# Fewer, larger transfers for the experts of a mixture-of-experts layer: two weight loads a part, one load of all biases, one output store, and a reordered hand-over

## The chip, the cores and the metric

The kernel runs on one core of one Trainium2 chip. Its time is device time in microseconds (us) of one execution, the median of several runs. A core has a matrix engine (TensorE, PE; its weight loads are listed as PEld), a vector engine (VectorE, DVE), a scalar engine (ScalarE, ACT), GpSimd (POOL) and a queue engine (SyncE, SP), each with its own instruction stream, and 16 DMA engines, which are fed from queues of SP, ACT and POOL. "Tile" below is a buffer in on-chip memory; "PSUM" is the memory that PE writes to.

## The reference

The input x has 32 images of 56 x 56 tokens of 128 channels, in float32. It goes through a binarised 3 x 3 convolution with group and batch normalisation, a windowed causal attention with 4 heads, and a mixture-of-experts layer in which every expert chooses its tokens. The change touches only this last layer:

```
logits = einsum('bsd,ed->bse', x, gate_w) + gate_b
probs = softmax(logits, axis=1)                       # over the 3136 tokens of an image
vals, idx = top_k(probs.transpose(0, 2, 1), K)        # 64 experts, K = 8 tokens each
gathered = take_along_axis(x, flat_idx[:, :, None], axis=1)
pooled = einsum('bked,bke->bed', gathered, topv)      # one vector per image and expert
h = gelu(einsum('ebd,edh->ebh', [pooled, 1], weight1))  # 512 hidden values
out = einsum('ebh,eho->ebo', [h, 1], weight2)
weighted = einsum('beo,bke->bkeo', out, topv)
outputs = zeros.at[batch, flat_idx].add(weighted)     # added onto the layer's input
```

x is the layer-normalised input here. A token that several experts of one image chose gets the sum of their outputs. weight1 is 64 x 129 x 512 and weight2 is 64 x 513 x 128; the last row of each is the bias. Together they are 33.6 MB.

## The kernel before

**Main loop.** The images are taken in 16 pairs (NPAIR), and the tokens of a pair in 7 blocks, so that there are N = 112 blocks. One loop over n runs the whole chain (load, convolution, normalisation, attention, projection) as a pipeline written out by hand: in one turn different blocks are at different stages. Each engine's order is the order of the code, apart from waits on semaphores. The normalised tokens of a pair are stored to `toks` in DRAM, the layer's residual to the output.

**Choosing tokens.** As soon as a pair's blocks are through, `Pair.step(j)` runs one step a block: `spread` sends the inverse deviations through DRAM into `drow` (a row per expert), `scale` multiplies the logits by them, `largest` and `tokens` take the 8 largest and their indices (`idx`, `idxf`) and store them (`slots`, `putrow`), `gather` fetches the 8 token rows with eight indirect DMAs of POOL into `rows`. `row_stats` stores these rows to `grows` in DRAM with 16 DMAs on SP (L804), computes their statistics, and loads `srow`, the indices of all experts of the image in each partition (L817). `weigh` makes the weighted sum `g_acc` of the rows, which `turn_pooled` and `pool` turn into `pooled`. `shares` compares `srow` with a slot's index, eight times (L854, L859): how much each expert adds to the token of each slot. `store_shares` stores this to `share` in DRAM by a DMA of POOL. `put_rows` loads `rowidx`, the output rows of all slots.

**Hand-over.** For the last pair these steps come after the loop, one behind the other, with the first loads for the experts among them.

**Experts.** The 64 experts are taken in 16 groups of 4 (NG, EG), two groups to a part, 8 parts (NQ). `Group(g, pool)` loads the group's weights on SP: four DMAs of 256 KB for u1 (L353), four for u2 (L355), four of 16 KB for the biases u3 (L360). The pools `early` and `late` hold two groups each, so four groups, two parts, are in flight; group g + 4 is loaded at the end of `outputs(g)`. For a part q the code runs:

- `hidden(g)`: hp = pooled x u1, 16 products (L1019); ACT copies it to `hs` (L1024);
- `gelus(g)`: transposes (L1030) and 32 activations with the first bias (L1035);
- `outputs(g)`: op = hT x u2 (L1047), DVE adds the second bias into `os` (L1054), ACT stores it to `eout` in DRAM (L1055), and after the second group loads the part's outputs back into `eo` in an order by image (L1061). `eo` lies in a tile named logits, and the profile calls it so;
- `finals(q)`: for each pair fo = share x eo (L1072), DVE adds it to the token rows `f_rows` (L1077), and 16 indirect DMAs of POOL scatter them into the output (L1081).

`finals(q - 1)` stands between `gelus` and `outputs` of part q. `load_rows` (L1005) and `load_shares` (L1013) bring a part's `f_rows` and `f_sh` from `grows` and `share`, two parts ahead.

Scatters of one pair stay in the order of the parts. POOL, PE, DVE, ACT and SP otherwise wait only for data and for buffers.

Of the kernel before, what the change touches and what calls it, by code (L numbers as in the profile page):

```python
# [17 lines left out]
P = 128  # L18
# [3 lines left out]
K = 8  # L22
# [8 lines left out]
def kernel(  # L31
# [303 lines left out]
    grows = dram.tile([NQ, P, NPAIR, P], F32, name="grows")  # L335
# [8 lines left out]
    class Group:  # L344


        def __init__(self, g, pool):
            self.e0 = g * EG
            self.u1 = pool.tile([P, EG, HF], F32, name="u1")
            self.u2 = pool.tile([P, EG, NHC, P], F32, name="u2")  # L350
            self.bias = pool.tile([P, P], F32, name="u3")
            for e in range(EG):
                nc.sync.dma_start(out=self.u1[:, e, :], in_=weight1[self.e0 + e, 0:C, :])  # L353
            for e in range(EG):
                nc.sync.dma_start(  # L355
                    out=self.u2[:, e].rearrange("p c o -> p (c o)"),
                    in_=weight2[self.e0 + e, 0:HF, :].rearrange("(p c) o -> p (c o)", c=NHC),
                )
            for e in range(EG):
                nc.sync.dma_start(  # L360
                    out=self.bias[e * B : (e + 1) * B],
                    in_=weight2[g * EG + e, HF : HF + 1, :].to_broadcast([B, P]),
                )
# [3 lines left out]
    def main_loop(fast):  # L367
        with ExitStack() as main:
# [7 lines left out]
            early = main.enter_context(tc.tile_pool(name="early", bufs=2))  # L376
# [324 lines left out]
            class Pair:  # L701
# [48 lines left out]
                def tokens(self):  # L750
# [18 lines left out]
                    nc.sync.dma_start(out=slots[pr], in_=self.idxf)  # L769
                    nc.sync.dma_start(out=putrow[pr], in_=pidx)  # L770
# [28 lines left out]
                def row_stats(self):  # L799

                    pr, rows = self.pr, self.rows
                    for i in range(2):
                        for q in range(NQ):
                            nc.sync.dma_start(  # L804
                                out=grows[q, i * ES : (i + 1) * ES, pr, :].rearrange(
                                    "(e k) c -> e k c", k=K
                                ),
                                in_=rows[i * E + q * EP : i * E + (q + 1) * EP],
                            )
# [4 lines left out]
                    self.srow = wp.tile([P, E, K], F32, name="srow")  # L814
                    for i in range(2):
                        half = slice(i * E, (i + 1) * E)
                        nc.sync.dma_start(  # L817
                            out=self.srow[half].rearrange("p e k -> p (e k)"),
                            in_=slots[pr][half].rearrange("(o e) k -> o (e k)", o=1).to_broadcast([E, E * K]),
                        )  # L820

                def weigh(self):

                    rows, st = self.rows, self.st
                    rtot = wp.tile([P, 1], F32, name="rtot")
                    nc.vector.reciprocal(rtot, self.tot)
                    nc.vector.tensor_scalar(self.topv, self.topv, rtot, None, ALU.mult)
# [49 lines left out]
                def step(self, j):  # L877
# [11 lines left out]
                    elif j == 6:  # L889
                        self.row_stats()  # L890
                    elif j == 7:
                        self.weigh()
# [20 lines left out]
            for n in range(-6, N + 1):  # L913
# [12 lines left out]
                if n == N - 4:  # L926
                    groups = [Group(g, early) for g in range(2)]
# [31 lines left out]
                for j, pair in steps:  # L959
                    pair.step(j)  # L960
# [19 lines left out]
            def pool(name, bufs, space=None):  # L980
# [4 lines left out]
                pool(name, bufs) for name, bufs in (("late", 2), ("eh", 2), ("frow", 4), ("fsh", 1))  # L985
# [11 lines left out]
            sync_dep = mybir.DependencyInfo(mybir.DependencyClass.Sync, mybir.DependencyReason.DATA)  # L997

            def load_rows(q, n0, n1):
# [3 lines left out]
                for a in range(n0, n1, FP):  # L1003
                    b = min(a + FP, n1)
                    nc.sync.dma_start(out=rows[q][:, a:b], in_=grows[q][:, a:b])  # L1005

            def load_shares(q, n0, n1):
                shs[q] = shbuf[q % 3]
                for i in range(2):
                    part = slice(i * E, (i + 1) * E)  # L1010
                    for a in range(n0, n1, 2 * FP):
                        b = min(a + 2 * FP, n1)
                        nc.sync.dma_start(out=shs[q][part, a:b, i, :], in_=share[q][part, a:b])  # L1013

            def hidden(g):
                group = groups[g]
                hp = eps.tile([P, HF], F32, name="hp")
                for e in range(EG):
                    nc.tensor.matmul(  # L1019
                        hp[e * B : (e + 1) * B, :], lhsT=pooled[:, group.e0 + e, :],  # L1020
                        rhs=group.u1[:, e, :], start=True, stop=True,
                    )
                hs[g] = eh.tile([P, HF], F32, name="hs")
                nc.scalar.copy(hs[g], hp)  # L1024

            def gelus(g):
                hT_ps = eps.tile([P, NHC, P], F32, name="hT_ps")
                hc = hs[g].rearrange("p (m c) -> p c m", c=NHC)
                for c in range(NHC):
                    nc.tensor.transpose(hT_ps[:, c, :], hc[:, c, :], ident)  # L1030
                hT[g] = eh.tile([P, NHC, P], F32, name="hT")
                for c in range(NHC):
                    for e in range(EG):
# [159 lines left out]
```

## Time and profile before

| | us |
|---|---|
| median of 3 runs (lowest and highest) | 2401.21 (2399.71 to 2408.39) |
| profiled execution | 2529.53 |
| its span in the profile | 2527.7 |
| main loop, about | 280 to 2150 |
| hand-over | 2170 to 2244 |
| experts, from the first fo to the end | 2244 to 2528 |
| start of `finals` of parts 0 to 7 | 2243.7, 2277.9, 2311.5, 2344.9, 2384.3, 2427.3, 2471.0, 2497.7 |
| busy in the span: PE, DVE, ACT, POOL | 2198.1, 1770.1, 1166.8, 812.6 |

All times within the kernel are from one profiled execution, counted from the start of its span. It is 128 us longer than the median of the runs. In the views, a row of waits reads: engine and line that waited, "<-", the engine and the line (or the DMA) that ended the wait, the sum in us, how often, the longest. Rows of SPq, ACTq and POOLq are the DMA issues of a queue: start, how long the issuing took, line, target and source, number.

### The profile page before, as it was taken

What the parts mean: (1) busy time and instruction counts of PE and PEld (TensorE: products, weight loads), DVE (VectorE), ACT (ScalarE), POOL (GpSimd) and SP (SyncE); (2) the same over time, 40 slices, a digit from 0 to 9 for tenths busy, and PEclk for the clock granted to TensorE, in tenths of its full rate; (3) what the DMA queues carried; (4) which work ended last, traced back from release to release, by engine and by line L of the source; (5) the groups of instructions that cost most, each with busy time, mean ns of one, the idle gap of its engine ahead of it and who ended that gap; (6) DMA issues with size and microseconds to landing.
All of it is one profiled execution on the core that took longest, in us unless ns stands there. A gap on an engine that the chain in (4) does not pass through costs nothing.

```text
span 2527.7 us, 83568 instructions
## 1 busy us (share of the span) xinstructions
PE 2198.1 (87%) x35852; PEld 1527.2 (60%) x35852; DVE 1770.1 (70%) x4955; ACT 1166.8 (46%) x1699; POOL 812.6 (32%) x761
## 2 busy tenths in 40 slices
PE   6769999999999999999999999999999999234433
PEld 5647676666666666666666666666666666123212
DVE  8965577878787878787878787878788787621101
ACT  0015555555555555555555555565555554122211
POOL 1011223232424242423333333333232424324434
PEclk9989999999999999999999999999999999667766
DMA  9932344443435353434343435353534445755552
GB/s 374 391 108 55 94 108 104 105 113 95 122 87 137 79 130 83 126 86 126 92 117 93 125 88 133 77 132 82 126 91 117 100 108 141 193 163 181 168 152 83
DMA packets 272749, 321.22 MB, mean 127 GB/s; under 512 B 74801, under 2 KB 214257, under 8 KB 270321
## 3 DMA queue, kind: packets, MB, share of 16 engines
q1 hardware_dynamic: 240496, 241.29, 34.1%
q0 software_dynamic: 27392, 72.38, 11.4%
q8 instruction: 285, 4.67, 0.8%
q10 hardware_dynamic: 4480, 2.10, 0.3%
q14 instruction: 96, 0.78, 0.1%
HBM read 190.35 MB, written 125.31 MB: 125 GB/s over the span
## 4 chain that ended last, share of the span: by engine, by line
PE 71%; issue 10%; ACT 7%; POOL 6%; DVE 6%; DMA 0%; POOLq 0%; SPq 0%; another core or an unknown queue 0%; DVEq 0%
PE cv L503 8%; PE av L633 8%; PE kT_ps L544 8%; PE pj L667 7%; PE v_ps L560 7%; PE sc L584 6%; POOL out_dram L1081 4%; PE xT_ps L434 4%; PE lg L695 4%; PE yt L434 4%; ACT bn L482 4%; PE rr L531 4%; PE tt L434 3%; ACT xT L474 3%; DVE st L301 3%
## 5 line engine op out<-in xcount | busy, mean ns | idle before, releaser
L420 POOL TENSOR_TENSOR ln_rstd<-ln_var,nhalf 128x7 f32<-128x7 f32 x112 | 167.6, 1497 | 946.1 <-DVE ln_var L417 607.7
L474 ACT ACTIVATE xT<-xT_ps,conv_nb 128x896 f32<-128x896 f32 x112 | 112.8, 1007 | 401.6 <-PE xT_ps L434 401.6
L420 POOL TENSOR_TENSOR devs<-ln_var,nhalf 128x7 f32<-128x7 f32 x112 | 165.8, 1480 | 267.5 <-DVE ln_var L417 267.5
L503 PE MATMUL cv<-hbits,wconv 128*128 128x448 f16 x1008 | 236.3, 361 | 12.4 <-DVE s L518 6.3
L599 ACT ACTIVATE pT<-sc 128x896 f32<-128x896 f32 x224 | 193.3, 915 | 115.8 <-PE sc L584 115.8
L633 PEld LDWEIGHTS av<-vblk,pT 64*64 64x64 f32 x12544 | 194.4, 135 | 80.1 <-ACT pT L599 72.9
L560 PEld LDWEIGHTS v_ps<-wqkvT,n1T 128*128 128x128 f32 x1568 | 192.7, 192 | 41.6 <-issue 41.6
L633 PE MATMUL av<-vblk,pT 64*64 64x33 f32 x12544 | 207.6, 221 | 0.8 <-ACT pT L599 0.5
L673 DVE SCALAR_TENSOR_TENSOR tT<-pj,bproj_c,yT 128x448 f32<-128x448 f32 x224 | 142.7, 679 | 92.7 <-PE pj L667 70.9
L516 ACT ACTIVATE s<-cv,conv_mid 128x448 int32<-128x448 f32 x112 | 70.8, 632 | 295.9 <-PE cv L503 219.6
L544 PE MATMUL kT_ps<-n1T,wqkvT 128*128 128x448 f32 x448 | 197.8, 564 | 4.4
L667 PE MATMUL pj<-aoT,wprojT 64*128 64x448 f32 x896 | 200.3, 566 | 1.1 <-ACT aoT L659 1.1
L560 PE MATMUL v_ps<-wqkvT,n1T 128*128 128x128 f32 x1568 | 193.1, 275 | 0.0
L544 PE MATMUL qT_ps<-n1T,wqkvT 128*128 128x448 f32 x448 | 187.7, 542 | 0.0
L427 DVE BATCH_NORM_STATS2 ln_st<-yt 128x6 f32<-128x128 f32 x784 | 165.6, 285 | 22.0 <-PE tt L434 9.6
L1081 POOL DMA_INDIRECT out_dram<-f_rows,rowidx x128 | 123.8, 967 | 165.7 <-DVE f_rows L1077 129.1
L584 PE MATMUL sc<-qT,kT 32*64 32x64 f32 x12544 | 172.0, 237 | 2.1 <-issue 2.1
L584 PEld LDWEIGHTS sc<-qT,kT 32*64 32x64 f32 x12544 | 156.0, 133 | 25.8 <-issue 25.7
L686 POOL DMA_DIRECT2D out_dram<-tok x224 | 169.3, 757 | 0.0
L427 DVE BATCH_NORM_STATS2 ln_st<-tok 128x6 f32<-128x128 f32 x784 | 161.9, 281 | 5.2 <-ACT tok L681 5.2
L482 ACT ACTIVATE bn<-xT_ps,thr_b,thr_a 128x448 f32<-128x448 f32 x224 | 149.2, 720 | 3.1 <-DVE thr_b L330 2.6
L520 DVE SCALAR_TENSOR_TENSOR yT<-s,conv_s,xT 128x448 f32<-128x448 f32 x224 | 143.5, 682 | 4.0
(183 smaller groups left out, 4105.3 us busy)
## 6 DMA issues: line engine op xcount, KB each, us to landing
xb<-in_x_dram SPq DMA_DIRECT2D x16, 3136.0 KB
xb<-in_x_dram SPq DMA_DIRECT2D x224, 224.0 KB
toks<-tok SPq DMA_DIRECT2D x224, 224.0 KB
out_dram<-tok POOLq DMA_DIRECT2D x224, 224.0 KB
u<-in_L_ffn_weight_dram SPq DMA_DIRECT2D x128, 256.0 KB
drow<-devs SPq DMA_DIRECT2D x224, 112.0 KB
grows<-rows SPq DMA_DIRECT2D x256, 32.0 KB
f_rows<-grows SPq DMA_DIRECT2D x30, 256.0 KB
```

What stands on the lines that cost most here:

```text
L420: nc.gpsimd.tensor_tensor(rstd, var, nhalf[:, :n], ALU.pow)
L427: nc.vector.bn_stats(st[:, u, :], src[:, u, :])
L434: nc.tensor.transpose(units(t)[:, u, :], src[:, u, :], ident)
L482: nc.scalar.activation(bn[:, i].rearrange("c h (g j) -> c h g j", j=NU), units(xT_ps)[:, :, i * WIN : (i + 1) * WIN].rearrange("c j (h g) ...
L503: nc.tensor.matmul(self.cv[:, :BT], lhsT=wconv[:, t, :], rhs=hb[:, r * RB + kh : r * RB + kh + RB, kw : kw + W], start=(t == 0), stop=(t = ...
L544: nc.tensor.matmul(pp[:, a, :BT], lhsT=wqkvT[:, s, :], rhs=flat[:, a * BT : (a + 1) * BT], start=True, stop=True,)
L560: nc.tensor.matmul(units(vp)[:, u, :], lhsT=self.n1T[:, u, :], rhs=wqkvT[:, 2, :], start=True, stop=True,)
L584: nc.tensor.matmul(tiles[h // 2][part, h % 2, u * WIN : (u + 1) * WIN], lhsT=left[hp, u, part], rhs=right[hp, u, part], start=False, stop= ...
L599: nc.scalar.activation(pT, rows2(sc), AF.Exp, scale=HD ** -0.5)
L633: nc.tensor.matmul(av[h % 2 * WIN : (h % 2 + 1) * WIN, i, m * VW : (m + 1) * VW], lhsT=self.pT[h // 2][rows, h % 2, u, :], rhs=self.vb[row ...
L667: nc.tensor.matmul(pj[:, i, :BT], lhsT=wprojT[rows, g, :], rhs=self.aoT[rows, :, g, :], start=(g == 0), stop=(g == 1),)
L1081: put = nc.gpsimd.indirect_dma_start(out=of, out_offset=bass.IndirectOffsetOnAxis(ap=rowidx[:, n, q : q + 1], axis=0), in_=rows[q][:, n, : ...
```

## The change

- **Weights.** `Part(q, pool)` takes the place of `Group`. It loads a part's u1 in one DMA of 2 MB and its u2 in another. Each of the pools `early` and `late` holds one part. u1 of part q + 2 is issued after `hidden(q)`, u2 after `outputs(q)`.
- **Biases.** All second biases are loaded once, with four DMAs in the hand-over, into `obias`, which lies in the buffer of `drow`.
- **Outputs.** `hidden`, `gelus` and `outputs` take a part. `os` holds both groups and is stored to `eout` by one DMA of 128 KB.
- **Rows and shares.** `grows` is laid out by slot, and a pair's rows are stored in one DMA, for every pair. A part's `f_rows` come in two DMAs, with runs of up to 8 KB, its `f_sh` in two.
- **Last pair.** In the last turn of the loop the steps of the pairs run in reverse order. In the hand-over `slot_rows` (the load of `srow`) follows the store of `slots` at once; five of the eight shares come before the weighted sum; three after `hidden(0)`; most memsets of POOL come ahead of the gathers; `put_rows` comes last. `probabilities` holds two instructions that were in `weigh`.

```
-    grows = dram.tile([NQ, P, NPAIR, P], F32, name="grows")
+    grows = dram.tile([P, K, NPAIR, P], F32, name="grows")
...
+    class Part:
+        def __init__(self, q, pool):
+            self.q, self.pool = q, pool
+        def load1(self):
+            self.u1 = self.pool.tile([P, EP, HF], F32, name="u1")
+            es = slice(self.q * EP, (self.q + 1) * EP)
+            nc.sync.dma_start(out=self.u1, in_=weight1[es, 0:C, :].rearrange("e c h -> c e h"))
+        def load2(self):
+            self.u2 = self.pool.tile([P, EP, NHC, P], F32, name="u2")
+            es = slice(self.q * EP, (self.q + 1) * EP)
+            nc.sync.dma_start(
+                out=self.u2.rearrange("p e c o -> p e (c o)"),
+                in_=weight2[es, 0:HF, :].rearrange("e (p c) o -> p e (c o)", c=NHC),
+            )
...
                     nc.sync.dma_start(out=slots[pr], in_=self.idxf)
+                    if pr == NPAIR - 1:
+                        self.slot_rows()
                     nc.sync.dma_start(out=putrow[pr], in_=pidx)
...
-                    for i in range(2):
-                        for q in range(NQ):
-                            nc.sync.dma_start(
-                                out=grows[q, i * ES : (i + 1) * ES, pr, :].rearrange(
-                                    "(e k) c -> e k c", k=K
-                                ),
-                                in_=rows[i * E + q * EP : i * E + (q + 1) * EP],
-                            )
+                    nc.sync.dma_start(out=grows[:, :, pr, :], in_=rows)
...
                 if n == N - 4:
-                    groups = [Group(g, early) for g in range(2)]
+                    parts = [Part(0, early)]
+                    parts[0].load1()
+                    parts[0].load2()
...
-                for j, pair in steps:
+                for j, pair in steps if n < N else steps[::-1]:
                     pair.step(j)
...
+                for i in range(2):
+                    es = slice(i * E + q * EP, i * E + (q + 1) * EP)
+                    nc.sync.dma_start(
+                        out=rows[q][i * ES : (i + 1) * ES, n0:n1],
+                        in_=grows[es].rearrange("e k n c -> (e k) n c")[:, n0:n1],
+                    )
...
+            def outputs(q):
+                part = parts[q]
+                os = eh.tile([P, GQ, P], F32, name="os")
+                for g in range(q * GQ, (q + 1) * GQ):
...
+                    for e in range(EG):
+                        one = slice(e * B, (e + 1) * B)
+                        nc.vector.tensor_add(os[one, g % GQ], op[one, e % 2, :], obias[one, g])
+                es = slice(q * EP, (q + 1) * EP)
                 nc.scalar.dma_start(
-                    out=eout[group.e0 : group.e0 + EG].rearrange("e b o -> (e b) o"), in_=os
+                    out=eout[es].rearrange("(g e) b o -> (e b) g o", e=EG), in_=os
                 )
...
-                if g + 4 < NG:
-                    groups.append(Group(g + 4, early if g % 4 < 2 else late))
...
+            parts[1].load1()
+            parts[1].load2()
             pair.scale(NB - 1, NB)
             pair.largest(NB - 1, NB)
+            nc.gpsimd.memset(eo, 0.0)
+            zeros(0)
+            zeros(1)
             pair.tokens()
             pair.gather()
-            pair.put_rows()
-            pairs[NPAIR - 2].shares(range(2, 8))
-            pairs[NPAIR - 2].store_shares()
-            for q in range(2):
+            other.shares(range(2, 8))
+            other.store_shares()
+            for q in range(3):
                 load_rows(q, 0, N1)
-                load_shares(q, 0, N1 - 1)
+            obias = wp.tile([P, S], F32, name="drow")[:, : NG * P].rearrange("p (g o) -> p g o", o=P)
+            for e in range(EG):
+                nc.sync.dma_start(
+                    out=obias[e * B : (e + 1) * B],
+                    in_=weight2.rearrange("(g e) h o -> e h g o", e=EG)[e, HF : HF + 1]
+                    .to_broadcast([B, NG, P]),
+                )
             pair.exps()
+            pair.probabilities()
+            pair.shares(range(0, 4))
             pair.row_stats()
+            pair.shares(range(4, 5))
+            zeros(2)
             pair.weigh()
...
             pair.turn_pooled(eps.tile([P, 2, P], F32, name="pl", tag="op")[:, 0, :])
             pair.pool()
+            for q in range(3):
+                load_rows(q, N1, NPAIR)
             hidden(0)
-            hidden(1)
-            pair.shares(range(0, 4))
+            pair.shares(range(5, 8))
             gelus(0)
-            gelus(1)
-            pair.shares(range(4, 8))
             pair.store_shares()
+            pair.put_rows()
             gpsimd.close()
             outputs(0)
-            outputs(1)
-            for q in range(2):
-                load_shares(q, N1, NPAIR)
-            load_shares(2, 0, NPAIR)
+            parts[2].load1()
+            for q in range(3):
+                load_shares(q, 0, NPAIR)
+            parts[2].load2()
             for q in range(1, NQ + 1):
+                if q < NQ:
+                    hidden(q)
+                    if q + 2 < NQ:
+                        parts[q + 2].load1()
+                    gelus(q)
                 finals(q - 1)
                 if q + 2 < NQ:
                     load_shares(q + 2, 0, NPAIR)
+                if q < NQ:
+                    outputs(q)
                 if q + 2 < NQ:
+                    parts[q + 2].load2()
                     load_rows(q + 2, 0, NPAIR)
```

## The prediction

> **What bounds the kernel now.** I read the page's 40 slices first, then a table by stage, then the waits of the experts' stage, then the queue of SP. The slices show TensorE full until slice 34 and mostly idle after it:
>
> ```profile
> PE   6769999999999999999999999999999999234433
> ```
>
> Up to about 2150 us a change to DMA issues on SP can hardly show: PE is 90% busy or more in every slice from the fourth to the 34th. The change can only pay (or cost) in the last 360 us. The table by stage (busy us of PE, PEld, DVE, ACT, POOL, then clock, DMA share, GB/s) takes the hand-over and two parts of experts:
>
> ```profile
> 2170.00:2244.00 74.00, 15.79 (x83) 7.50 (x84) 40.34 (x79) 17.01 (x67) 19.88 (x20) 0.59 0.77 213
> ...
> 2278.00:2312.00 34.00, 15.11 (x90) 10.35 (x91) 5.06 (x12) 6.31 (x33) 15.46 (x16) 0.70 0.58 176
> ...
> 2384.00:2427.00 43.00, 17.78 (x90) 8.27 (x89) 5.06 (x12) 6.90 (x36) 15.47 (x16) 0.72 0.58 171
> ```
>
> The second part does the same work as the first one shown and takes 43 us instead of 34, with no engine and no DMA full. So it waits. The chain of waits, in order of time, shows where: after a part's 16 scatters (16 x 1.27 = 20.3 us) POOL stands idle, 13.1 us before an early part, 22.8 before a late one:
>
> ```profile
> 2334.60 13.13 issue
> ...
> 2406.36 22.80 issue
> ```
>
> The sum of waits (2140 to 2528) gives the names:
>
> ```profile
> ACT hs L1024 <- DMA logits<-eout: 129.3, 5, 28.2
> POOL out_dram L1081 <- DVE f_rows L1077: 129.1, 8, 23.6
> DVE f_rows L1077 <- PE fo L1072: 105.4, 20, 18.6
> DVE os L1054 <- remote: 97.0, 10, 13.0
> PEld hp L1019 <- DMA u<-in_L_ffn_weight_dram: 85.7, 20, 19.9
> ```
>
> Each part runs os, the store eout, the loads eo (named logits), fo, f_rows, scatters, one after the other; in late parts hp also waits for weights, up to 19.9 us. Why weights are late stands in the waits of SP's own queue:
>
> ```profile
> SPq L355 <- DMA eout<-os: 25.2, 2, 13.3
> SPq L353 <- DMA eout<-os: 23.1, 3, 18.6
> ```
>
> The built program gives the DMAs of SP and ACT eight semaphores in turn, so a weight load on SP can stand behind a 64 KB eout of ACT. With 36 such DMAs a part this happens in every part; the timeline of SP shows one burst held 19 us:
>
> ```profile
> 2322.67 19.08 SPq L360 DMA_DIRECT2D u<-in_L_ffn_weight_dram  x4
> ```
>
> The hand-over has its own queue: 16 small row stores ahead of srow on SP, and DVE idle for it:
>
> ```profile
> 2204.18 12.09 SPq L804 DMA_DIRECT2D grows<-rows  x16
> 2216.38 1.14 SPq L817 DMA_DIRECT2D srow<-slots  x2
> ```
>
> DVE idles 12.97 us for srow (to 2220.41), then makes eight shares, and only then os.
>
> [...] from the end of eo's issue to the first fo are 3.4 us in a quiet part (2308.05 to 2311.5), 6.0 us (2237.66 to 2243.66) beside weights at a DMA share of 0.95. [...] with 256 KB loads queued, the DMA view of 2228 to 2244 already shows slices of 400 to 415 GB/s. The gain from few DMAs must come from waits and issue, not from rate. [...] eout on ACT measures less, 1.3 us from the end of its issue (2305.42) to eo's (2306.69).
>
> **The change part by part**, against the profiled execution (2529.5 us, span 2527.7).
>
> 1. **Main loop: 0** (-5 to +5). grows falls from 16 DMAs (12.09 us of issue) to one, the first part's weights from 24 to 2. Both are issue time on SP, which PE's 90% and more hides. The cover goes only if SP came last for a block's loads; no view shows it. The bytes stay. The 4 MB behind n = N - 4 now stand as one piece ahead of the toks stores of that block, which are needed some 50 us later (three blocks of 17).
>
> 2. **Hand-over: -9** (-15 to 0). SP's weights of part 1 took 2173.80 to 2187.10, and slots was issued at 2187.85 though idxf was ready at 2183.6. Two DMAs (about 1 us) go before slots now, and srow follows it at once: it lands near 2191 instead of 2220. Its data stand behind the 4 MB in the rings: at 400 GB/s that is 10.5 us, to about 2185. The reversed steps let the last pair's scale fill the 2.87 us in which DVE waits for pl before 2170.70: idx about 1.5 us earlier. Against this, five shares (0.55 each, and 0.69 for each addition) now stand ahead of the row statistics, and the first must wait until pair 14's share store, issued on POOL behind eight gathers (2194.3, now about 2193), has landed, about 2196. Shares to 2200.5, eight statistics 2.3, variance 0.5, POOL's power 1.7, weights 0.6, g_acc 3 us (4.8 before, beside POOL's memsets, most of which now go ahead of the gathers): pooled near 2208.5, against 2207.15, +1.3 (0 to +4). From pooled on, PE and ACT are as before: op ended at 2219.2 and os could have run; it began at 2229.91, behind srow and the shares, 10.6 us late. Three shares are left (3.7 us), under the gelus (5.8 us). os: -10.6 + 1.3 = -9.3. Behind os stands the weight stream as before (u2 of part 2 in place of groups 4 and 5), so eout, eo and fo follow as before.
>
> 3. **Late parts: -24** (-30 to -8). The stalls before the scatters were 18.1, 22.8 and 23.4 us in the parts with late weights, 13.4 in those without (13.8, 13.4, 13.1): 4.7 + 9.4 + 10.0 = 24.1. With 9 DMAs a part instead of 36, u1(q+2) is issued as soon as hidden(q) has read its buffer and u2(q+2) after outputs(q), each more than a part ahead of need: 5.2 MB of weights and rows at 400 GB/s are 13 us, in a part of over 30. Taken whole, u1 makes the first hp wait for 2 MB instead of 256 KB; that is covered as long as SP runs those parts ahead.
>
> 4. **The stream beside eout and eo: +15** (0 to +35). What is late next: the chain os, eout, eo, fo. In parts 1 to 3 the held SP kept the rings empty in just that stretch (its weights began at 2310.44, after eo's issue at 2306.69). Now outputs(q) releases u2(q+2), f_rows(q+2) and then u1(q+3): 5 MB, 13 us from there, beside eout and eo of the same part. The two readings above give +2.6 for eo; eout beside the stream (2232.7 to 2235.7) 3 instead of 1.3, +1.7; less where it overlaps in part only (part 5: eo issued 2412.10 to 2413.47, its u stream already on). I take +3 for the five parts with loads left. f_rows now has runs of 8 KB instead of 2 KB; how an 8 KB piece delays eo this trace does not show in that place, hence the upper end of 7 a part.
>
> 5. **Edits at nothing.** Biases at once: 64 DMAs of 16 KB gone from SP, whose issue lies beside other work once the stalls of 3 are gone; obias takes drow's buffer, free since 2178. One eout of 128 KB for two of 64: the first lay under other work, the second takes at most 0.5 us longer. f_rows and f_sh in two DMAs each: their issue is on SP only. memsets on POOL: in its idle time before the gathers. Tail: last fo to the end stays 30 us (16 scatters and 7 us of landing and close).
>
> Sum in the profiled execution: 0 - 9 - 24 + 15 = **-18**. The median (2401.2) is 128 us below the profiled execution, and the trace cannot say where. One place is likely: os waits 97.0 us for op's matmuls ("remote"), which come late while POOL scatters. If unprofiled parts lack that, they sit nearer the scatters' 20.3 us, and half of the +15 is covered by these: -25. I take **-25: 2376**.
>
> **Rivals.** (a) My forecast, 2376, own range 2362 to 2389. (b) Weights were late in more parts than the profile shows, since shorter unprofiled parts leave SP less time: stalls of 9 us in six parts, 54, and the hand-over, 9, less the 7 of the stream: 56, of which the scatters keep some: near 2350. For it: the stall grows from part to part; against: none in parts 1 to 3. (c) The stream costs 5 us in five parts and eats the late parts' gain: only the hand-over is left, 2392. (d) **Slower**: eout and eo, whose chain ends last in every part, stand beside f_rows' 8 KB pieces and 2 MB loads; ACT waits in order, so hs and the gelus of the next part stand behind it. From (24 + 9 + 12) / 5 = 9 us a part it makes the kernel slower by over 0.5%; at 10.5 us it gives +20, 2421. For it: 129.3 us of ACT's waiting is already for eout; against: 6.0 us was the worst seen beside a full stream. That the change doesn't do what it says I leave out: the built program has nine hardware DMAs a part.
>
> **How the numbers follow.** A measurement can tell 0.5%, 12 us, from no change. Chances: (a) 0.50, (b) 0.20, (c) 0.14, (d) 0.16. (a) and (b) are faster: 0.70; (c) is the same: 0.14; (d) slower: 0.16. The range takes (a), most of (b) and (c) and the near end of (d): 2340 to 2408; (a)'s own stands above.
>
> **What would show it.** Right: srow landed before the gathers end; os of part 0 near 2220; hp without waits for u; SP without waits on eout; scatters of parts 4 to 6 spaced as those of parts 1 to 3, within 5 us. Eo to fo between 4 and 7 us instead of 3.4. Wrong: hp still waiting for u (the weights are late by bytes, not by semaphores); eo to fo above 9 us (d); spacing of 34 us in all parts with no stream seen (step 4 too dear); pooled later than 2212.

## The result, and the profile after

| | us, median (lowest to highest) | runs |
|---|---|---|
| before | 2401.52 (2398.40 to 2409.86) | 18 |
| after | 2411.49 (2407.56 to 2416.26) | 18 |

The ratio is 1.0039 (95% interval 1.0031 to 1.0047): 10 us slower, where 25 us faster was forecast. The profiled execution of after has a span of 2408.8 us.

One thing has to be known before any two numbers are compared: **the jobs differ.** The experiments ran in five jobs, each on a chip of its own, and before took 2504.7, 2537.2, 2535.6, 2401.6 and 2400.8 us in them. So three jobs are slower and two faster, and by their times the 36 runs above go with the faster. The profile of before that the forecast was read from took 2529.5 us. The record does not name its chip; that it goes with the slower jobs is inferred from its time and from its waits, which the first experiment repeats. Each chip was used in one job only, so no run shows whether the difference lies in the chip or in something else of the job: "slower job" and "faster job" below say what before took there and no more, and "a chip of the slow kind" in the expectations is such a job. Numbers are compared within a job, or between traces of slower jobs or of faster ones, and where not, it is said.

The slices of the profile after, PE:

```profile
PE   6769999999999999999999999999999999924642
```

The idle end is 5 slices of 60 us here, and was 6 of 63. The table by stage (columns as before): hand-over, and two parts.

```profile
2120.00:2205.00 85.00, 19.63 (x94) 8.87 (x94) 41.92 (x92) 20.00 (x75) 22.50 (x21) 0.58 0.74 184
...
2233.00:2255.00 22.00, 13.36 (x90) 9.92 (x91) 5.06 (x12) 3.90 (x19) 14.45 (x15) 0.73 0.79 226
...
2306.00:2335.00 29.00, 13.82 (x88) 10.43 (x88) 5.06 (x12) 6.87 (x34) 15.46 (x16) 0.68 0.86 244
```

Parts take 22 to 29 us, not 34 to 44, but most of that goes with the job (after takes 28 to 39 for the same parts in a slower one). DMA share is 0.79 to 0.86 where it was 0.58, at 226 to 244 GB/s. The sum of waits (from 2117; the row "hs" is ACT's first work of the next part, which stands behind eo in ACT's order):

```profile
DVE f_rows L1088 <- PE fo L1083: 143.0, 32, 20.1
ACT hs L1035 <- DMA logits<-eout: 123.0, 7, 24.5
```

No row "hp <- DMA u" is left; 85.7 and 67.0 us of it were there before. One wait of 0.9 us is put down to weights, at fo. But ACT still waits 123 us for eout and eo. The chain of waits says how long each takes:

```profile
2150.59 11.07 DMA share<-sh
...
2197.26 7.78 DMA f_sh<-share
...
2215.81 7.02 DMA eout<-os
2223.62 9.26 DMA logits<-eout
```

The last two rows are part 1: 16 us for two small transfers one after the other. The issues of the same two, in a quiet part of before and in part 1 of after:

```profile
2305.09 0.33 ACTq L1055 DMA_DIRECT2D eout<-os  x1
2306.69 1.36 ACTq L1061 DMA_DIRECT2D logits<-eout  x2
```

```profile
2215.81 0.37 ACTq L1070 DMA_DIRECT2D eout<-os  x1
2222.90 1.39 ACTq L1074 DMA_DIRECT2D logits<-eout  x2
```

From the start of eout's issue to eo's issue are 7.1 us, from there to the first fo 10.3 (2233.23). In before, whose trace goes with the slower jobs, they were 1.6 and 4.8 (to 2311.5), for an eout of half the bytes. The first two rows of the chain are the hand-over. And SP's queue still stands:

```profile
SPq L1023 <- DMA logits<-eout: 39.5, 4, 20.1
SPq L353 <- DMA eout<-os: 30.0, 2, 15.7
SPq L776 <- DMA eout<-os: 13.1, 1, 13.1
```

The eight semaphores are still shared by SP and ACT: in the records of after, 900 DMAs of SP and 24 of ACT carry the same eight (in before 1348 and 32). With fewer DMAs SP stands behind eout and eo as long as before (106 us in all the rows of that kind, 99 in before), in other places: at f_sh, at u1, and in the hand-over 13.1 us at rowidx (L776), with u1 of part 2 and f_sh behind it.

### The profile page after: what moved, and what is told of

It is laid out like the page before. It is cut to its first block, busy times and chain, and to the rows that moved or that the text cites. A ratio compares the mean times of both kernels' runs of the same rounds, so it can differ in the third digit from the quotient of the medians.

```text
span 2408.8 us, 83035 instructions
## 1 busy us (share of the span) xinstructions
PE 2166.0 (90%) x35852; PEld 1525.5 (63%) x35852; DVE 1764.8 (73%) x4955; ACT 1168.0 (48%) x1699; POOL 812.9 (34%) x761
## 4 chain that ended last, share of the span: by engine, by line
PE 75%; ACT 8%; DVE 5%; POOL 4%; DMA 3%; issue 3%; SPq 1%; POOLq 0%; ACTq 0%; DVEq 0%
PE cv L501 8%; PE av L631 8%; PE kT_ps L542 8%; PE pj L665 8%; PE v_ps L558 7%; PE sc L582 7%; PE xT_ps L432 4%; PE yt L432 4%; PE lg L693 4%; ACT bn L480 4%; PE rr L529 4%; PE tt L432 3%; ACT xT L472 3%; DVE st L301 3%; POOL out_dram L1092 3%
## 5 line engine op out<-in xcount | busy, mean ns | idle before, releaser
L671 DVE SCALAR_TENSOR_TENSOR tT<-pj,bproj_c,yT 128x448 f32<-128x448 f32 x224 | 142.7, 679 | 85.7 <-PE pj L665 85.7
```

## The experiments

**First job, slower (before 2504.7).**

*The kernel before, again.* No edit.

> The kernel before, profiled once more. Theory A (its first profiled execution was not typical: in it every matmul beside an indirect DMA of POOL was late, and the stalls of parts 4 to 6 came with that): span near 2401, no block of the main loop above 18.5 us, parts of 20 to 28 us, and os without long 'remote' waits. Rival (profiling this kernel always costs it 128 us): span near 2529 again, blocks of 19 to 22 us after each gather.

2507.9 us, among the 2496.2 to 2521.6 of the other runs of before in this job. The rows of its waits repeat the first profile's:

```profile
PEld hp L1019 <- DMA u<-in_L_ffn_weight_dram: 85.3, 21, 18.6
DVE os L1054 <- remote: 78.5, 8, 13.1
```

The rival has the number, but not the reason: the first profile is like a slower job's, and this profiled execution is as long as the timed ones. "Remote" is what the view prints when it finds no instruction close to the moment at which the semaphore rose. In the first profile os starts 1.7 to 17.4 us after the recorded end of op's last product in parts 1 to 7, where POOL scatters beside it; in after, which scatters too, it is at most 0.1 us. Read here as: op was done late. The ends of matmuls are modelled, so the records do not show that itself.

*Own buffer for the last sum of shares.*

```
-                        self.sh = wp.tile([P, E, K], F32, name="sh")
+                        if self.pr == NPAIR - 1:
+                            self.sh = self.spare
+                        else:
+                            self.sh = wp.tile([P, E, K], F32, name="sh")
...
+            old = wp.tile([P, S], F32, name="drow")
+            obias = old[:, : NG * P].rearrange("p (g o) -> p g o", o=P)
+            pair.spare = old[:, NG * P : NG * P + E * K].rearrange("p (e k) -> p e k", k=K)
```

> The kernel after, with the last pair's sum of shares in a buffer of its own (the unused end of drow's), so that its first share need not wait for the store of pair 14's shares. Theory B (the hand-over's loss is that wait, 12.8 us on DVE ahead of the row statistics): pooled about 10 us earlier, 2399 to 2405 against 2411. Rival (finals of part 0 are ended by f_sh anyway, whose DMAs stand in SP's queue behind others): pooled earlier but the first fo moves by under 4 us, 2408 to 2412.

2450.2 us, 0.979 of before (0.9744 to 0.9836). The expectation's 2411 does not hold for this job, and after itself was not in this job; what can be read is the trace: pooled starts 47.6 us after the last product of a projection (pj, from here on the mark of this stage) instead of 55.9, the first fo 77.7 instead of 86.3 (against the trace of after from the result; after's traces of a slower and of a faster job agree within 1 us in this stage). Theory B holds for 8.6 us of the hand-over.

*After, without the weight stream.* `parts += [parts[q % 2] for q in range(2, NQ)]`, and no load1 and load2 for them.

> The kernel after, but parts 2 to 7 take the weights of parts 0 and 1 again: 25 MB of weight loads are left out, and the outputs of those parts are not the reference's. Theory C (the weight stream beside the 64 KB transfers of ACT is what lengthens the parts: eout 6.7 us to land instead of 1.3, eo 8.9 instead of 3.4): both fall back to 1.3 to 2 and 3 to 4, parts 1 to 6 near the scatters' 20.3 us, 25 to 35 us less: 2376 to 2386. Rival (lanes: small DMAs wait for their turn on the semaphores, not for bytes): under 8 us less, 2403 or more.

2453.2 us (0.9784; 0.974 to 0.9827). Taking 25 MB of loads away left the parts at 28 to 34 us. From the first fo of part 0 to that of part 7 are 200.0 us, and 196.7 in the kernel with its own buffer, of the same job, which has the loads. In this job something else sets the parts, so nothing is decided on theory C here.

*Before, without the weight stream.* `groups.append(groups[g])` in place of the loads.

> The kernel before, but groups 4 to 15 take the weights of groups 0 to 3 again (25 MB of loads left out, outputs not the reference's). If late weights stall the parts of the kernel before outside the first profile too (my forecast), 20 to 40 us less: 2360 to 2380. If its parts already ran near the scatters' rate and only the stream beside eout and eo cost a little, 5 to 15 us less: 2386 to 2396.

2464.2 us (0.9835; 0.9795 to 0.9876): 40 us less. The late parts' stalls that the forecast read are real in this job: from the first fo of part 4 to those of parts 5 and 6 are 33.6 and 27.3 us, where before's trace of this job has 43.9 and 43.8.

**Second job, slower (before 2537.2).**

*After again.* No edit.

> The kernel after, unchanged, beside the kernel before on the chip of this job. In the job of the first four experiments the kernel before took 2504.7 us, [...] where it took 2401.5 us the kernel after took 2411.5. If this job's chip is of the slow kind (before near 2500): after near 2455, 2% faster. If of the other kind (before near 2401): 2411 again.

2492.0 us, ratio 0.9824 (0.9774 to 0.9875). In a slower job the change is 1.8% **faster**.

*Two weight DMAs a part, alone*, in the kernel before.

```
-            for e in range(EG):
-                nc.sync.dma_start(out=self.u1[:, e, :], in_=weight1[self.e0 + e, 0:C, :])
+            nc.sync.dma_start(out=self.u1, in_=weight1[es, 0:C, :].rearrange("e c h -> c e h"))
```

> The kernel before with one edit: a part's weights in two DMAs of 2 MB, issued after the part's outputs; biases by group, rows, shares, outputs and hand-over as before (24 weight and bias DMAs a part become 10). Theory A (few DMAs free SP from the stalls of late parts): in a chip of the slow kind 20 to 30 us less than before; in the other kind nothing or 5 less. Theory C (a whole 2 MB stream meets eout and eo): in the other kind 5 to 20 us more.

(u2 likewise; the two are issued one after the other, after the part's outputs.) 2510.4 us (0.991; 0.9875 to 0.9945), 27 us less: theory A's number for such a job.

*Mended hand-over.* The own buffer, and:

```
             other.store_shares()
+            pair.put_rows()
...
+            for q in range(3):
+                load_shares(q, 0, N1)
             hidden(0)
...
-            pair.put_rows()
             gpsimd.close()
+            for q in range(3):
+                load_shares(q, N1, NPAIR)
             outputs(0)
             parts[2].load1()
-            for q in range(3):
-                load_shares(q, 0, NPAIR)
             parts[2].load2()
```

> The kernel after with a mended hand-over: own buffer for the last pair's sum of shares, rowidx loaded before the f_rows, shares of 15 pairs loaded before hidden(0), and those of the last pair ahead of the 2 MB load of u1. Theory B (the hand-over cost the time: 12.8 us for the share store ahead of the statistics, then SP 13.1 us behind eout and fo 10.2 us for f_sh): the first fo 15 to 20 us earlier than after's, and the kernel 15 to 20 us faster than after (0.6 to 0.8%). Rival (parts are bound by the weight stream from the start, so an early fo only waits in part 1): under 6 us.

2472.8 us (0.9771; 0.9731 to 0.9811), 19 us less than after. The first fo comes 68.2 us after the mark instead of 85.3. That is theory B, within its range.

*Old order of the hand-over*, in the kernel after.

> The kernel after with the order of before's hand-over (srow behind the row store, eight shares after the statistics, rowidx and f_sh where they were), its transfers and its experts' loop kept. If the reordered hand-over is the loss: 5 to 10 us faster than after. If the order itself gains (9 us by my forecast): 5 to 10 us slower than after.

2504.9 us (0.9884; 0.9823 to 0.9946), 13 us more than after, with ranges that overlap (2493.4 to 2523.1 against 2478.0 to 2502.3); the first fo at 87.8 us, 2.5 more. The new order is not the loss. In the hand-over it gains 2.5 us with the new transfers; the mended hand-over shows that waits which it need not have cost it 17.

**Third job, slower (before 2535.6): plain stores in place of the indirect scatters.** To see the parts without what the slower jobs add, the scatters were replaced in four kernels:

```
-                    put = nc.gpsimd.indirect_dma_start(
-                        out=of, out_offset=bass.IndirectOffsetOnAxis(ap=rowidx[:, n, q : q + 1], axis=0),
-                        in_=rows[q][:, n, :], in_offset=None,
-                    ).ins
...
+                    r0 = 2 * n * S + q * P
+                    nc.gpsimd.dma_start(out=of[r0 : r0 + P], in_=rows[q][:, n, :])
+                    nc.gpsimd.memset(filler, 0.0)
```

The memset was to keep POOL's pace; it ran beside the issue, so that a part's stores take 14.7 us in most parts instead of 20.0. Two things go along with the edit: the order that the scatters of one pair had among the parts is left out, and POOL keeps its hand-written order to the end of the experts.

*Before, plain stores.*

> The kernel before with the experts' 128 indirect scatters of POOL replaced by 128 plain stores of the same bytes to fixed rows (the output is not the reference's), each followed by a memset of 128x448 that keeps POOL's pace near 1.27 us. Theory D (what differs between chips is that matmuls beside an indirect DMA of POOL come late): on a chip of the slow kind 70 to 90 us less than before, os without 'remote' waits, parts of 20 to 28 us. Rival (any DMA of POOL beside PE does it, or DMA load): under 20 us less.

2435.8 us (0.9598; 0.9564 to 0.9632): 100 us less. os no longer waits for "remote":

```profile
DVE os L1055 <- PE op L1048: 11.9, 14, 1.2
```

So in the slower jobs os waits long for "remote" beside POOL's indirect DMAs (78.5 us in before's trace of the first job), and not beside plain stores. That is what theory D expects, with a gain 10 us above its range; that it is the matmuls that come late stays a reading. Some 7 us of it may be POOL's quicker pace: that is what after gains from plain stores in faster jobs (2411.5 to 2404.4, different jobs). hp still waits for weights, 51.1 and 27.4 us.

This kernel is still 35 us above the 2401 of the faster jobs. What is left lies in the main loop: 1954 us here, 1904 to 1907 in after and its variants in faster jobs. The loop's gathers are indirect DMAs of POOL too, and were left in place. In five traces of slower jobs, this one among them, a block with a gather in it takes 18.0 to 18.8 us on average; in two of faster ones it takes 17.1. Blocks without a gather take 17.2 us in both. The granted clock of the loop is 0.99 to 1.00 in both; in the blocks with a gather it is 0.98 in the first profile and 1.00 in after, which by estimate is 0.3 us of the 1.3 between their 18.4 and 17.1 us, so the clock is not most of the difference.

*After, plain stores.*

> The kernel after with the same replacement of its scatters. It stands for what the change does where matmuls beside the scatters are not late. If the result (0.4% slower) comes from that alone: this 5 to 15 us slower than the kernel before with direct stores. If the chip has some other influence: faster than it, by 20 us or more.

2448.7 us: 13 us more than before with plain stores (2447.3 to 2450.5 against 2432.7 to 2444.9). The sign of the result is back in a slower job, with the scatters replaced in both. The traces of the pair place less than half of it. From the first fo of part 0 to that of part 7: 165.4 us before, 167.3 after; the first fo 83.6 and 85.7 us after the mark; up to the mark 1.7 more; the end alike. That is 5.7 us in sum. The traced run of before was the slowest of its four (2444.9; the others 2432.7 to 2436.3), so where the other 7 us lie is not known. The loop over the parts gained nothing.

*Mended hand-over, plain stores.*

> The kernel after with the mended hand-over (own buffer for the last sum of shares, rowidx first, shares of 15 pairs early, those of the last ahead of u1) and the replaced scatters. Theory B: the first fo 15 to 20 us earlier than in the kernel after with direct stores, of which 10 to 18 are left at the end. Rival (the stream bounds the first parts): under 5 left.

2433.6 us, 15 us less than after with plain stores. Its first fo, beside that of after with plain stores:

```profile
2233.71 5.88 PE L1087 MATMUL fo<-logits,f_sh 128*128 128x128 f32 x32 [2.81 <-DMA logits<-eout]
```

```profile
2254.64 5.46 PE L1084 MATMUL fo<-logits,f_sh 128*128 128x128 f32 x32 [10.58 <-DMA f_sh<-share]
```

In the second row PE waits 10.58 us for f_sh; in the first, for eo. Of the 17.6 us by which fo is earlier in its stage, 15 are left by the medians. By the traces it is 11 or 12: part 1 takes 29.5 us instead of 23.2, so that a third of the gain waits there, as the rival has it, and 3.3 us of the difference in span lie in the main loop, which the edit does not touch.

*After, plain stores, without the weight stream.*

> The kernel after with the replaced scatters and with parts 2 to 7 taking the weights of parts 0 and 1 again (25 MB of loads left out, output not the reference's). Theory C (eout and eo beside the stream: 6.7 and 8.9 us instead of 1.3 and 3.4): eout and eo at 1.3 to 2 and 3 to 4 us, parts at POOL's 20.3 us, 20 to 30 us less than the kernel after with direct stores. Rival (POOL bounds the parts already): under 8 us less.

2413.8 us, 35 us less: above theory C's range. Of the 38 us between the two traced runs 24.0 lie between the first fo of part 0 and that of part 7 (143.3 instead of 167.3) and 6.6 in the hand-over, where u1's load stands ahead of f_sh; the other 7.5 lie in the main loop, which the edit does not touch. So the stream costs the parts 24 us. In detail theory C holds by half: eo comes back to between 3.2 and 3.6 us, while eout is still slow:

```profile
2251.08 0.37 ACTq L1072 DMA_DIRECT2D eout<-os  x1
2257.05 1.39 ACTq L1076 DMA_DIRECT2D logits<-eout  x2
```

5.6 us from the end of eout's issue to eo's, with no weights in the queues, only f_rows and f_sh. In the trace's packet records eout's first packet leaves 4.0 us after its issue began; in a quiet part it is 0.9. So part of the delay comes before eout has moved anything: it does not start. No weights are needed for this: in parts 1 to 5 some 730 to 850 KB of f_rows were outstanding on SP (issued, but their packets not yet begun) when eout was issued; in part 6 nothing was, and eout began after 0.9 us.

**Fourth job, faster (before 2401.6).**

> The kernel after with direct stores, unchanged, as the mark in this job for the two kernels above: 2440 to 2455.

2404.4 us, 1.0012 of before (1.0 to 1.0023). The expected range was one for a slower job.

*Weight loads cut into eight*, at the same place, in after with plain stores.

```
-            nc.sync.dma_start(out=self.u1, in_=weight1[es, 0:C, :].rearrange("e c h -> c e h"))
+            for e in range(EP):
+                nc.sync.dma_start(out=self.u1[:, e, :], in_=weight1[es.start + e, 0:C, :])
```

> The kernel after with direct stores in place of the scatters, each weight load of 2 MB cut into eight of 256 KB at the same place in SP's order (16 weight DMAs a part instead of 2). If the size of a DMA keeps ACT's small transfers waiting (eout 6 to 9 us to land in the kernel after, 3.4 to 5.2 and 1.4 in the kernel before, both with direct stores): eout back to 2 to 5 us, 10 to 25 us less than the kernel after with direct stores. If it is only the time at which the bytes are released: eout as late as with two DMAs, within 6 us of it, or slower because SP stalls again on the shared semaphores.

(u2 likewise.) 2393.6 us, 10.9 less than its mark. Part 1 of it and of its mark:

```profile
2217.17 0.37 ACTq L1073 DMA_DIRECT2D eout<-os  x1
2219.52 1.38 ACTq L1077 DMA_DIRECT2D logits<-eout  x2
```

```profile
2215.46 0.37 ACTq L1071 DMA_DIRECT2D eout<-os  x1
2222.91 1.39 ACTq L1075 DMA_DIRECT2D logits<-eout  x2
```

2.0 us against 7.1. Over parts 1 to 6 eout lands after 4.2 us on average, against 7.2, and its first packet leaves after 2.2 instead of 3.8. It is tempting to call size the cause, but the edit changes two things. SP stands at the shared semaphores between the pieces (24.0 us behind eo, 13.9 and 8.3 behind eout at the weight loads), so that less is outstanding when eout is issued. In part 1 only 58 KB of SP's were, in part 3 44 KB, against 816 KB or more in every one of these parts of the mark; in both eout began after 0.9 us. Part 5, with 1142 KB outstanding, most of it in pieces of 256 KB, is nearly as slow as in the mark: eout lands after 5.6 us, against 6.7, and its first packet leaves after 3.7, against 3.8:

```profile
2306.21 0.37 ACTq L1073 DMA_DIRECT2D eout<-os  x1
2312.13 1.37 ACTq L1077 DMA_DIRECT2D logits<-eout  x2
```

The packet records of fifteen traces of after and its variants, with the eouts of 8 parts each, say the same. Of 57 eouts with at most 250 KB outstanding on SP, every one began 0.9 to 1.3 us after its issue. Of 58 with 700 KB or more, 57 began after 1.4 to 5.1 us and one after 1.0: behind large DMAs after 3.7 on average (45 cases), behind weights in pieces of 256 KB after 3.0 (8 cases), with f_rows and f_sh in pieces too after 2.4 (5 cases). **So eout is late where SP has much outstanding, and the size of the DMAs has the smaller part in it.** This is read from traces; no run changes the one without the other. hp waits for u again (31.1 us), and the kernel is faster all the same.

*Release behind eo.* With the mended hand-over, and with u1 of part 2 issued ahead of the first outputs, u2 and u1 wait on SP behind a DMA that reads eo:

```
+                if q + 1 < NQ:
+                    nc.sync.dma_start(out=seen[q - 1], in_=eo[(q - 1) * EP : P : E, 0, 0:1])
+                    parts[q + 1].load2()
+                if q + 2 < NQ:
+                    parts[q + 2].load1()
```

> Mended hand-over, direct stores, two weight DMAs a part, and one edit more: u2 of part q+1, u1 of part q+2 and what follows on SP wait behind a DMA of two values that reads eo of part q-1, so that the stream starts when eo has landed, not when outputs has run. If the release beside eout and eo is the cost: eout 1.3 to 2 us, eo to fo 3.2 to 4, parts 18 to 22 us, 15 to 30 us less than the mended hand-over alone. If the bytes of a part (5.7 MB, some 15 us at full rate) do not fit between eo and the next eout: under 8 us less, with hp or op waiting for u.

2388.7 us: 16 less than the mark, and the mended hand-over alone gave 15 in the third job, so that no gain of the release itself is seen. eout still takes 6.7, 7.3 and 6.6 us in parts 1 to 3. The edit did not reach its aim there: 2846, 1966 and 1850 KB were outstanding on SP when eout was issued. In part 4 none were, and eout took 1.8 us, but eo met the next weights instead and took 9.4. So a part's bytes did not fit between eo and the next eout, and what an empty queue for both would be worth no run shows.

*The same with the scatters.*

> The same with the indirect scatters in place: a full kernel. On a chip of the slow kind[...] it should stand with the mended hand-over (2.3% faster than before) or 5 us below; on the other kind 25 to 40 us below the kernel before.

2394.6 us (0.9973; 0.9964 to 0.9982): 7 us better than before, not the 25 to 40 expected.

**Fifth job, faster (before 2400.8).**

> A full kernel: the kernel after with the mended hand-over and with each weight load in eight DMAs of 256 KB. The two gains measured apart with direct stores are 15 us (hand-over) and 11 us (size of the weight DMAs). On a chip where the kernel before takes 2401: after's 2411 less 26, 2385, 0.7% faster than before. If the gains overlap (the stream is released no later, only the chain before it is shorter): 2395, 0.3%. On a chip of the slow kind: 2.3 to 2.8% faster than before.

**2382.9 us (0.9929; 0.9916 to 0.9943)**: 18 us faster than before, and 2 us below the 2385 that the two gains give in sum. This kernel beats both. Its chain in part 1, which took 7.02 and 9.26 us in after:

```profile
2198.24 5.63 DMA eout<-os
...
2204.66 5.41 DMA logits<-eout
```

*f_rows and f_sh in pieces too* (four and eight pairs to a DMA).

> The same with f_rows and f_sh in pieces of the kernel before too (four pairs, eight pairs a DMA; 8 f_rows and 4 f_sh DMAs a part). Without the weight stream eout still took 5 to 6 us to land beside f_rows and f_sh in two DMAs each; if their size holds it up too, eout lands in 2 to 4 us and this is 5 to 10 us faster than the kernel above. If SP's stalls on the shared semaphores come back with 30 DMAs a part: the same or up to 10 us slower, with hp waiting for u.

2386.3 us (0.9943; 0.993 to 0.9957), 3.4 more than without: eout lands after 4.8 us on average in parts 1 to 6, no sooner than without this edit (4.7). In its trace the first fo comes 4.7 us later than without the edit, so that the loss lies mostly in the hand-over. Nothing speaks for cutting f_rows and f_sh.

## Why the prediction was wrong

Two steps failed: step 2, which put the landing of a store at 3 us and two loads at nothing, and step 4, whose price for the weight stream was too low. And the sum was added to a median that has another bound.

- **Step 1, main loop, 0: nothing speaks against it.** From the first to the last projection the kernel before takes 1948 and 1934 us in slower jobs, after 1955 in one; traces of the same kernel in such jobs differ by as much. In faster jobs after and its variants take 1904 to 1907, and there is no profile of before.
- **Step 2, hand-over, -9: it was +2 to +4.** srow came as early as forecast (issued 28.4 us after the mark instead of 55.5), and idx 1 us earlier. The term that failed is the landing of pair 14's share store: taken as some 3 us, it took 11.07. Even in the trace of before, its last packet began 5.4 us after the start of its issue. In the trace's packet records of after its pieces run among those of 3 MB of f_rows, 7.7 KB each, which the reordering issues in this stretch; that they are the reason no run singles out. The first share waited 12.8 us, pooled came 10 us later instead of 1.3, os 3 to 5 us earlier instead of 9.3. Then "eout, eo and fo follow as before" failed: rowidx stood 13.1 us behind eout's semaphore, u1's 2 MB and f_sh behind rowidx, and fo waited 10.2 us for f_sh. I costed f_sh at nothing ("their issue is on SP only") and rowidx not at all, and looked for stalls on the shared semaphores only where they had been before. Mending these waits gave 15 to 19 us.
- **Step 3, late parts, -24: right in kind.** hp never waits for u in after. Two weight DMAs alone gave -27 in a slower job, and before without its loads -40. What step 3 is worth in the job of the result was not measured.
- **Step 4, the stream beside eout and eo: the term that was mis-sized.** +3 in five parts, +15 in all; the stream costs the parts 24 us in the pair of traces with plain stores. The step named the right thing: in before SP, held at its semaphores, had at most 10 KB outstanding when the second eout of each of parts 1 to 5 was issued. But its price takes for granted that ACT's small transfers are only slowed while SP's stream moves beside them. That was the author's assumption; the two readings of eo in before (3.4 and 6.0 us) did not show it. In part 1 of after eout's first packet leaves 3.6 us after its issue began, and eo is issued 3.5 us after that; in part 7, with nothing outstanding, the two are 0.9 and 1.0.
- **The sum does not close.** Steps 3 and 4 as -24 and +24 cancel, which is what the pair with plain stores shows (+1.9 over the parts), and step 2 adds 2 to 4. That is +2 to +4, against +13 in the medians of that pair and +10 in the result. The direction follows; the rest of the size stays open.
- **The profile and the median.** The 128 us between them were no cost of profiling that hides somewhere, but by all signs what sets the slower jobs apart. The hunch about "remote" waits was right: the traces of faster jobs have none. What I drew from it, that shorter parts cover half of the stream's +15, was the wrong way round. In the slower second job os is late, SP's queue has drained when eout is issued (nothing outstanding in parts 2 to 6 of after), and eout lands after 1.5 to 1.8 us. There the change is 1.8% faster, 45 us, more than the -18 summed from that profile. In after's trace from the result os is early, 556 to 2328 KB are outstanding in parts 1 to 6, and eout takes 4.8 to 7.7 us. For the job of the median the profile showed the wrong bound.

Rival (d) named what happened in the parts: eout and eo beside f_rows and the 2 MB loads. Its threshold, 9 us a part, counted on the hand-over's -9; with +3 there, step 3's 24 us are used up at about 4 us a part, and 24 us over six parts are that much.

Open: why os waits for "remote" beside indirect DMAs in some jobs (44 to 97 us) and not in others; why after's parts are shorter than before's in such jobs even without weight loads (mostly 28 to 29 us against 33); why ACT's eout starts late (2.7 to 4.1 us in after) when SP has much outstanding; and how the 10 us of the result divide between hand-over and parts in the very job where it was measured, of which there is no profile of before.

## What to carry to other kernels

Ask of large transfers what starts while they are outstanding: here a small one on another queue, on which a chain waits, sent its first packet 2.7 to 4.1 us after its issue began instead of 0.9. Fewer DMAs are no end in themselves; waits of the issuing engine that look like a loss may be what keeps the queue clear for a short chain, as here, where they left at most 10 KB outstanding in parts 1 to 5, and after had 556 to 2328 KB in parts 1 to 6. When a change takes such waits away, look for what they were holding back. And before adding a gain to a median, make sure that the profile and the median come from the same bound: a profiled time that is 5% off is a finding to be explained first.

## What was not expected of the hardware

- In the slower jobs os came late beside indirect DMAs of POOL: it has 44 to 97 us of "remote" waits in the nine traces there of kernels with scatters, the first profile counted in, and none in the four such traces of faster jobs. Plain stores of the same bytes from POOL removed these waits, and 100 us of the kernel before.
- An eout of 128 KB that ACT issues while SP has 700 KB or more outstanding sends its first packet after 1.4 to 5.1 us (one after 1.0), against 0.9 to 1.3 with 250 KB or less. In parts 1 to 6 of after, with 556 KB or more, it is 2.7 to 4.1; in its parts 0 and 7, with 2 KB or less, 0.9.
- Few DMAs were not short issues. Four bias loads with rows of 512 bytes held SP 7.67 us (L1122), 5.3 of them the third alone and 0.5 to 0.6 each of the others, while 3 MB of f_rows were on the way; the one row store of 512 KB held it 6.58 us (L802):

```profile
2152.03 7.67 SPq L1122 DMA_DIRECT2D drow<-in_L_ffn_weight_dram  x4
2160.01 6.58 SPq L802 DMA_DIRECT2D grows<-rows  x1
```
